# Pacing layer 0 further ahead of layer 1, and giving the ending steps of a tile pair a lower priority number, in a planned two-layer attention kernel

## The chip, the cores and the metric

The kernel runs on one core of one Trainium2 chip. Everything is float32. The metric is the device time of one execution in microseconds (us), as the median of several runs. A core has five instruction queues of interest here: PE (TensorE, matrix products; PEld are its weight loads), ACT (ScalarE, activation functions), DVE (VectorE), POOL (GpSimd) and SP (SyncE, which here only issues DMA transfers). Each queue executes its instructions strictly in the order in which the program issued them; queues wait for each other through semaphores.

## The reference

The input is 8 items (batch) of 64 x 16 positions with 128 channels, that is N = 1024 tokens of C = 128 per item. Two layers follow each other.

```python
# layer 0, per item: attention with 8 heads and two softmaxes in a row, then a feed-forward part
q, k, v = proj(wq), proj(wk), proj(wv)                    # 8 heads of 128
scores  = einsum('bhlfc,bhmgc->bhlfmg', q, k) / sqrt(128) # 1024 x 1024 per head
a = softmax(scores, axis=m); a = softmax(a, axis=g)       # over 64 rows, then over 16 columns
z = a @ v;  z1 = layer_norm(z @ wo.T + bo + x)
x = layer_norm(relu(z1 @ w1.T + b1) @ w2.T + b2 + z1)
# layer 1, per item: additive attention, then a recurrence over the tokens
Bn = ln(t);  Wi = Bn @ W.T
scores[i, j] = sum_d v[d] * tanh(Wi[i, d] + Wi[j, d])     # 1024 x 1024 x 128 tanh
t = t + softmax(scores, axis=j) @ Bn
Wx = batch_norm(ln(t) @ W);  y_t = sigmoid(Wx_t + y_{t-1} @ V.T)
out = t + y
```

Layer 1 of an item needs layer 0 of that item alone; only the batch normalisation and the recurrence at the very end need all 8 items.

## The kernel before, in words

**Two layers at once.** While layer 1 works on item b, layer 0 works on item b + 1. Layer 0 has 64 tiles per item (8 heads x 8 tiles of 128 queries). Tiles go in pairs. For each tile: score products on PE (L856), an exponential on ACT (L859), sums and reciprocals on DVE (L863, L864) and a division on DVE (L867). These *begin* a pair. Once per pair, the *ending* steps follow: one exponential over both tiles on ACT (L876, 128 x 2048), sums and reciprocals on DVE (L879, L880), a division on POOL (L890), four transposes through PSUM banks (L770 on PE, L782 on DVE), the product with the values (L904 on PE) and its addition to `zs` (L909 or L911 on DVE). There are two score buffers, and two pair buffers (`e`, with their statistics `stat_e`).

When the 64 tiles of an item are done, a serial chain ends layer 0: transposes, layer normalisation, the feed-forward part (L944, L950, L957, L963), a second normalisation, for both halves of the tokens. Then layer 1 begins: normalisation, a projection (L1085) and a copy into `wiT` (L1109), one per half.

**Rows.** Layer 1's bulk is `tanh(Wi[i] + Wi[j])` for all i <= j: 36 blocks of 128 x 128 pairs per item, since the scores are symmetric. The rows are made in groups of up to 4096 elements, in one of five slots `th`. A group is either made on ACT by itself (L999, `tanh` with the bias added), or the additions are made on POOL or DVE (L1009, L1003) and ACT applies one `tanh` to the group (L1045). PE multiplies each group by `v` into the tile `sa` (L1062). Block rows 0; 1 and 7; 2 and 6; 3 and 5; 4 are taken in this order (the first and the last item start with 4, 5 and 7, 6 instead, for which half of the tokens is enough). An exponential (L1158) empties `sa` after each, and attention steps with transposes and products (L1191) follow.

**The planner.** Nothing is issued directly. Each step is added to a `Plan` with an engine or several, a modelled duration, the keys that it reads and writes, and a priority number `pri`. `Plan.emit` then replays the program: it finds the earliest time at which any step could start, takes the steps that could start within 0.15 us of that on that engine, and issues the one with the lowest number. Engine order and the division of rows among ACT, POOL and DVE come out of that. The order is fixed when the program is built; the chip only follows it.

**The scale of the numbers.** One unit is one item of layer 1. The rows of item b have `ROWS` from b to b + 1. Layer 0 of item b has the number

```python
def pace(n_part, h):
    return b - 1 - LEAD + STRETCH * (n_part * H + h) / (len(parts) * H)
```

with `STRETCH` 0.95, or 1.25 for the last item. So tile by tile it runs from b - 1 - LEAD upwards: layer 0 of item b is on a par with the rows of item b - 1, `LEAD` units ahead. `L0` is set anew from `pace` for every tile. The chain that ends layer 0 has b - 1 - SOON and layer 1's normalisation and projection have b - SOON, with `SOON` 0.5, so both come ahead of the rows as soon as they can start. The product L1062 and the attention steps of layer 1 have `L1 = ROWS - LEAD`; the tanh of a group has ROWS - 0.02.

The DMAs stand apart: `load_xT` has b - 2, the parking of results follows layer 1's numbers, and `fetch_wx` has NB.

Of the kernel before, what the change touches and what calls it, by code (L numbers as in the profile page):

```python
# [413 lines left out]
class Plan:  # L414
# [24 lines left out]
    def add(self, where, fn, r=(), w=(), pri=0, mode="full", take=None, give=None, behind=(), wait=(), port=False):  # L439
        n = len(self.ops)  # L440
        deps = set()
        for k in r:
            if k in self.writer:
                deps.add(self.writer[k])
        for k in (*w, *wait):
            if k in self.writer:
                deps.add(self.writer[k])
            deps.update(self.readers.get(k, ()))
        for k in w:
            self.writer[k] = n  # L450
            self.readers[k] = []
        for k in r:
            if k not in w:
                self.readers.setdefault(k, []).append(n)
        deps.discard(n)
        self.ops.append((where, fn, (pri, n), mode, deps, take, give, behind, port))
        self.by.append(None)
        return n
# [107 lines left out]
def fast_path(ctx: ExitStack, tc: tile.TileContext, a: dict, fits):  # L566
# [150 lines left out]
    add = plan.add  # L717


    LEAD, SOON, LATE = 0.15, 0.5, -0.3  # L720

    stats = ring("stat", 7, [P, 4, 9])

# [36 lines left out]
    def through_bank(pe, weight, r, evict, where, more, w, pri, choice=two):  # L760

        bank = Bank(*choice)
        n = len(plan.ops)
        add(("PE", weight), lambda _: pe(bank()), r=r, w=[("bank", n)], pri=pri, take=bank, wait=more + w)
        add(where, lambda e: evict(e, bank()), r=[("bank", n)] + more, w=w, pri=pri, give=bank)

    def transposes(srcs):
        def fn(bank):
            for i, s in enumerate(srcs):
                nc.tensor.transpose(bank[:, i * P : (i + 1) * P], s, ident)  # L770

        return fn

    def copy(dst):
        def fn(e, bank):
            src = bank
            if len(dst.shape) == 3:
                src = bank[:, : dst.shape[1] * P].rearrange("p (t c) -> p t c", c=P)
            if e == "ACT":
                nc.scalar.activation(dst, src, AF.Copy)  # L780
            else:
                nc.vector.tensor_copy(dst, src)  # L782

        return fn
# [4 lines left out]
    def layer0(b):  # L789
# [13 lines left out]
        def pace(n_part, h):  # L803
            return b - 1 - LEAD + STRETCH * (n_part * H + h) / (len(parts) * H)

        for n_part, part in enumerate(parts):
# [3 lines left out]
            for h in range(H):  # L810
                L0 = pace(n_part, h)
# [29 lines left out]
                for qt in qts:  # L841
                    L0 = pace(n_part, h + (qt - qts[0]) / len(qts))
# [30 lines left out]


                    ks = [("e", pair, q) for q in range(2)]
                    add(("ACT", 1.9), lambda _, e2=e2: nc.scalar.activation(e2, e2, AF.Exp), r=ks, w=ks, pri=L0)  # L876

                    def second_sums(_, e2=e2, r2=r2):
# [42 lines left out]
            L0 = b - 1 - SOON  # L921
# [53 lines left out]

    def group(it, at0, r0, k, wiT, all_wi, L1, ROWS, fillers, chain, left, both, first_half):

# [80 lines left out]
        def times_v(_):  # L1058
# [15 lines left out]
            ("PE", k * (1.69e-3 * (w - begin[0]) + 0.005 * n)), times_v, r=[("tanh", g)] + before,  # L1074
            w=[("sa", it, r0)] + after, pri=L1, mode="groups", give=slot,
        )
        return ("sa", it, r0)

    def projected(src, ks, w, use, kw, L1, bT, kb):

        through_bank(
            transposes([src[:, i, :] for i in range(4)]), 0.52, ks, copy(bT), ("DVE", 0.7), [], [kb], L1
        )
        through_bank(
            lambda bank: nc.tensor.matmul(bank, w, bT, start=True, stop=True), 0.9, [kb], *use, [], [kw], L1  # L1085
        )
# [8 lines left out]
    def layer1(b):  # L1095
        L1 = b - SOON
        X, kX = Xs[b % NX], ("X", b % NX)
        B, kB = Bs[b % 2], ("B", b % 2)
        wiT, kw = wiTs[b % 2], ("wiT", b % 2)

        early = b in (0, NB - 1)
        for qh in (1, 0) if early else (0, 1):
            Xg, kg = X[:, 4 * qh : 4 * qh + 4, :], kX + (qh,)
            Bg = B[:, 4 * qh : 4 * qh + 4, 0:C]
            layer_norm(Xg, kg, Bg, kB + (qh,), 6, L1)

            def numbered(_, bank, qh=qh):
                dst = wiT[:, 512 * qh : 512 * qh + 512]
                nc.vector.tensor_copy(dst.rearrange("p (t r c) -> p t r c", t=4, c=4), bank.rearrange("p (t c r) -> p t r c", t=4, c=4))  # L1109


            at = wiT[:, 512 * qh : 512 * qh + 512]
            projected(Bg, [kB + (qh,)], wa_sb, (numbered, ("DVE", 0.75)), kw + (qh,), L1, at, kw + (qh,))
        all_wi = [kw + (1,), kw + (0,)]

        E_at = E_first
        fills = [("fill", False), ("fill", True)]
        order = ((4,), (5, 7), (6,), (0,), (1,), (2,), (3,)) if early else shared  # L1120
        done, attended = set(), set()
        past = 0
        for pair in order:
            todo = []
            for it in pair:
                w = N - it * P
                k = max(1, N // w)
                wide = it < NT // 2
                for r0 in range(0, 32, k):
                    late = r0 + 3 * k >= 32  # L1130
                    if wide:
                        fillers = [("ACT", 0.0)] + ([] if late else [("POOL", 0.0)])
                        if b == NB - 1:
                            fillers += [("DVE", 0.1)]
                    elif it == NT // 2:
                        fillers = [("DVE", 0.1), ("ACT", 0.1)] + ([] if late else [("POOL", 0.0)])
                    else:
                        fillers = [("DVE", 0.1)] + ([("ACT", 0.1)] if early else [("POOL", 0.0)])
                    todo.append((r0 + 0.5 * (not wide), it, 0 if it == pair[0] else N - pair[0] * P, r0, k, fillers))
            left = {}  # L1140
            n_blocks = sum(NT - it for it in pair)
            keys = []
            for s, it, at0, r0, k, fillers in sorted(todo):
                ROWS = b + (past + n_blocks * s / 33) / len(E_first) / 4.5
                L1 = ROWS - LEAD
                keys.append(group(it, at0, r0, k, wiT, all_wi[:1] if early and pair[0] >= NT // 2 else all_wi, L1, ROWS, fillers, fills[it < NT // 2], left, fills if r0 == 0 else (), b == 0 and pair[0] >= NT // 2))
            past += n_blocks
            blocks = [("E", it, j) for it in pair for j in range(it, NT)]

            runs = [pair] if not early else [(it,) for it in pair]  # L1150

            def exps(_, runs=runs):
                at0 = 0
                for run in runs:
                    w = sum(NT - it for it in run)
                    Ep = E_sb[:, E_at[run[0]] : E_at[run[0]] + w, :].rearrange("p t (c r) -> p t c r", c=4)
                    S = sa[:, at0 : at0 + w * P].rearrange("p (t r c) -> p t c r", r=32, c=4)
                    nc.scalar.activation(Ep, S, AF.Exp)  # L1158
                    at0 += w * P

            add(("ACT", 0.2 * len(runs) + 0.833e-3 * n_blocks * P), exps, r=["sa"] + keys, w=blocks, pri=L1)
            for it in pair:
                D, kD = E_sb[:, E_at[it], :], ("E", it, it)
                add(("DVE", 0.28), lambda _, D=D: nc.vector.tensor_tensor(D, D, half, ALU.mult),
                    r=[kD], w=[kD], pri=L1, port=True)
                through_bank(
                    transposes([D]), 0.25, [kD],
                    lambda _, bank, D=D: nc.vector.tensor_tensor(D, bank[:, :P], D, ALU.add),
                    ("DVE", 0.3), [kD], [kD], L1,
                )  # L1170
            done.update(pair)
            for it in range(NT):
                if it not in attended and done.issuperset(range(it + 1)):
                    attended.add(it)
                    attention(b, it, X, kX, B, kB, E_at, L1)
# [67 lines left out]
    def check_bounds():  # L1243
# [73 lines left out]
        add(("DVE", 1.7), compared, r=[("at1", 0), ("at1", 1)] + [("ET", j) for j in range(1, NT)], w=["fits"], pri=LATE)  # L1317

    layer0(0)
    check_bounds()  # L1320
    for b in range(NB):
        if b + 1 < NB:
            load_xT(b + 1)
            layer0(b + 1)
        layer1(b)
# [139 lines left out]
```

## Time and profile before

| what | value |
|---|---|
| median of 3 runs (lowest to highest) | 5696.39 us (5690.69 to 5700.09) |
| the profiled execution: its time, and its span | 5699.62 us, 5697.8 us |
| busy: ACT, PE, DVE, POOL (us of the span) | 5263.0, 5166.6, 4754.1, 4186.4 |
| mean granted TensorE clock | 0.975 |
| DMA | 37.82 MB, 7 GB/s in the mean |
| weight loads (PEld) | 2765.7 us, beside PE |

The span is the time from the first to the last instruction; the profiled execution's own time is 1.8 us more. Busy times of different engines overlap. The page also gives, for groups of equal instructions, the number, the busy time, the mean of one, and the idle time of the engine just before them with what ended it. A line number is that of the kernel's source; helpers such as the transposes at L770 are shared by both layers.

### The profile page before, as it was taken

The numbers are of one execution on the slowest core, as the hardware profiler recorded it, in microseconds if no ns is written. First come the engines' busy times: TensorE is split into PE (matmuls) and PEld (weight loads), VectorE is DVE, ScalarE is ACT, GpSimd is POOL, SyncE is SP. The second block draws the span as 40 slices with busy tenths as digits, with TensorE's granted clock in tenths as the row PEclk, the third lists the DMA queues.
The fourth block names the chain that finished last, engine by engine and source line by source line (L and its number), as shares of the span: only waits on it lengthen the run. The fifth ranks groups of instructions, "written<-read, shape, count | busy, mean of one in ns | idle before, by whom it ended". The sixth has DMA issues, their size and how long they took to land.

```text
span 5697.8 us, 97791 instructions
## 1 busy us (share of the span) xinstructions
PE 5166.6 (91%) x39013; PEld 2765.7 (49%) x39013; DVE 4754.1 (83%) x7545; ACT 5263.0 (92%) x4964; POOL 4186.4 (73%) x2678
## 2 busy tenths in 40 slices
PE   8899999899989999899998999989998999987567
PEld 6555455455544555445454455445454445543125
DVE  7989676778996889968898689986899669999886
ACT  5499999999998999899998999989998999999994
POOL 2362997788877888588796888868887886882882
PEclk9999999999999999999999999999999999998988
DMA  2000000000000000000000000000000000000001
GB/s 60 1 5 1 1 1 5 8 1 1 1 5 8 1 1 1 8 5 1 1 5 5 5 1 1 5 8 1 1 1 3 7 1 1 1 21 14 1 1 64
DMA packets 27330, 37.82 MB, mean 7 GB/s; under 512 B 2464, under 2 KB 19232, under 8 KB 26864
## 3 DMA queue, kind: packets, MB, share of 16 engines
q1 hardware_dynamic: 24832, 27.99, 1.5%
q8 instruction: 308, 5.05, 0.4%
q10 hardware_dynamic: 1872, 3.16, 0.2%
q14 instruction: 158, 1.29, 0.1%
q0 software_dynamic: 160, 0.33, 0.1%
HBM read 19.41 MB, written 12.06 MB: 6 GB/s over the span
## 4 chain that ended last, share of the span: by engine, by line
PE 40%; DVE 24%; ACT 23%; issue 4%; POOL 1%; DMA 0%; DVEq 0%; ACTq 0%; POOLq 0%
PE sa L1062 16%; ACT th L1045 10%; ACT th L999 9%; PE m L904 8%; PE sc L856 6%; PE m L770 4%; DVE th L1003 3%; DVE stat_e L879 3%; DVE th L1009 3%; DVE stat_e L863 2%; DVE aT L782 2%; ACT wx L876 2%; DVE wx L867 2%; ACT sc L859 2%; PE m L1191 1%
## 5 line engine op out<-in xcount | busy, mean ns | idle before, releaser
L1009 POOL TENSOR_TENSOR th<-wiT 128x896 f32<-128x896 f32 (+55 forms) x2088 | 3131.7, 1535 | 436.8 <-PE sa L1062 400.4
L1062 PE MATMUL sa<-th,vpat 128*32 128x512 f32 (+27 forms) x24576 | 2104.4, 466 | 223.6 <-ACT th L1045 212.6
L999 ACT ACTIVATE th<-wiT 128x516 f32<-128x516 f32 (+55 forms) x3044 | 2203.1, 798 | 37.1 <-DVE wiT L1109 21.1
L1045 ACT ACTIVATE th<-th 128x4096 f32<-128x4096 f32 (+54 forms) x766 | 2083.8, 2746 | 49.0 <-DVE th L1003 28.0
L890 POOL TENSOR_TENSOR wx<-wx,stat_e 128x1024 f32<-128x1024 f32 x512 | 998.3, 1971 | 755.9 <-DVE stat_e L880 527.5
L1062 PEld LDWEIGHTS sa<-th,vpat 128*32 128x32 f32 x24576 | 674.8, 111 | 1470.4 <-issue 834.4
L856 PE MATMUL sc<-xT,wx 128*128 128x512 f32 x2048 | 985.7, 606 | 36.0 <-DVE wx L867 35.8
L904 PE MATMUL m<-aT,wx 128*128 128x256 f32 x3584 | 862.2, 389 | 14.7 <-DVE aT L782 12.0
L1003 DVE TENSOR_SCALAR_CACHE_REDUCE th<-wiT 128x384 f32<-128x384 f32 (+47 forms) x1092 | 758.1, 694 | 86.3 <-PE sa L1062 15.0
L904 PEld LDWEIGHTS m<-aT,wx 128*128 128x128 f32 x3584 | 660.7, 191 | 238.9 <-issue 89.9
L782 DVE COPY aT<-m 128x512 f32<-128x512 f32 x927 | 598.2, 672 | 138.6 <-PE m L770 136.2
L863 DVE TENSOR_REDUCE stat_e<-sc 128x16 f32<-128x1024 f32 x512 | 620.1, 1211 | 101.1 <-ACT sc L859 99.9
L879 DVE TENSOR_REDUCE stat_e<-wx 128x128 f32<-128x2048 f32 x256 | 583.2, 2278 | 102.5 <-ACT wx L876 101.8
L867 DVE TENSOR_TENSOR wx<-sc,stat_e 128x1024 f32<-128x1024 f32 x512 | 623.4, 1218 | 23.8 <-DVE stat_e L864 0.5
L770 PE MATMUL m<-ident,wx 128*128 128x128 f32 x3932 | 571.9, 280 | 56.7 <-DVE aT L782 29.3
L770 PEld LDWEIGHTS m<-ident,wx 128*128 128x128 f32 x3932 | 434.9, 141 | 357.6 <-issue 164.2
L859 ACT ACTIVATE sc<-sc 128x1024 f32<-128x1024 f32 x512 | 513.1, 1005 | 92.3 <-PE sc L856 76.6
L876 ACT ACTIVATE wx<-wx 128x2048 f32<-128x2048 f32 x256 | 486.8, 1902 | 90.8 <-DVE wx L867 90.8
L856 PEld LDWEIGHTS sc<-xT,wx 128*128 128x128 f32 x2048 | 357.3, 192 | 367.1 <-issue 301.7
L1009 DVE TENSOR_TENSOR th<-wiT 128x1024 f32<-128x1024 f32 (+28 forms) x280 | 392.1, 1439 | 3.9 <-PE sa L1062 3.0
L880 DVE RECIPROCAL stat_e<-stat_e 128x128 f32<-128x128 f32 x256 | 243.9, 953 | 8.8
L738 POOL TENSOR_TENSOR stat<-stat,neg_half 128x4 f32<-128x4 f32 x64 | 65.3, 1020 | 245.4 <-DVE stat L735 230.6
(169 smaller groups left out, 3055.5 us busy)
## 6 DMA issues: line engine op xcount, KB each, us to landing
xT<-in_xt_dram SPq DMA_DIRECT2D x8, 512.0 KB, 3.7
th<-in_x_dram SPq DMA_DIRECT2D x8, 512.0 KB, 7.5
parked<-X SPq DMA_DIRECT2D x16, 256.0 KB, 2.3
xr<-parked SPq DMA_DIRECT2D x8, 512.0 KB, 8.3
parked_wx<-bT SPq DMA_DIRECT2D x14, 256.0 KB, 2.0
wx<-parked_wx SPq DMA_DIRECT2D x7, 512.0 KB, 3.3
out_dram<-ot ACTq DMA_DIRECT2D x8, 256.0 KB, 2.1
out_dram<-ot SPq DMA_DIRECT2D x8, 256.0 KB, 2.2
```

Of the source, the lines that this page charges most:

```text
L770: nc.tensor.transpose(bank[:, i * P : (i + 1) * P], s, ident)
L856: nc.tensor.matmul(sc[:, cols], u[:, qt * P : (qt + 1) * P], xT[:, cols], start=True, stop=True)
L863: nc.vector.tensor_reduce(r1, sc.rearrange("p (m g) -> p g m", g=G), AX.X, ALU.add)
L867: nc.vector.tensor_tensor(e3, sc3, r1.unsqueeze(1).to_broadcast([P, M, G]), ALU.mult)
L879: nc.vector.tensor_reduce(r2, e2.rearrange("p q (m g) -> p q m g", g=G), AX.X, ALU.add)
L890: nc.gpsimd.tensor_tensor(e3, e3, r2[:, q, :].unsqueeze(2).to_broadcast([P, M, G]), ALU.mult)
L904: nc.tensor.matmul(bank()[:, :256], vp[:, t, :], aT[:, t, :], start=t == 0, stop=t == NT - 1)
L999: nc.scalar.activation(rows(c)[:, r, :], wiT[:, i0 + begin[c] :], AF.Tanh, bias=w_i(c, r))
L1003: nc.vector.tensor_scalar(rows(c)[:, r, :], wiT[:, i0 + begin[c] :], w_i(c, r), 0.0, ALU.add, ALU.add, accum_out=unused)
L1009: eng.tensor_tensor(rows(c), wiT[:, i0 + begin[c] :].unsqueeze(1).to_broadcast(shape), w_i(c).unsqueeze(2).to_broadcast(shape), ALU.add,)
L1045: lambda _: nc.scalar.activation(slot()[:, : at[4]], slot()[:, : at[4]], AF.Tanh),
L1062: nc.tensor.matmul(sa[32 * c : 32 * c + 32, s:s1], vpat[:, 31 - r0 - r : 63 - r0 - r], rows(c)[:, r, s - at0 - begin[c] : s1 - at0 - begin ...
```

## The change

Layer 0's pace gets a lead of 0.35 in place of 0.15. Layer 1's products and attention steps keep ROWS - 0.15, now written as a number. The ending steps of a tile pair, from the exponential at L876 on, get a number lower by `DOWN` = 0.06 than the tile that they follow. No instruction is added or removed by the text of the change; the planner decides anew on the order, and on which engine adds which rows.

```diff
-    LEAD, SOON, LATE = 0.15, 0.5, -0.3
+
+    LEAD, DOWN, SOON, LATE = 0.35, 0.06, 0.5, -0.3
...
                     ks = [("e", pair, q) for q in range(2)]
+                    L0 -= DOWN
                     add(("ACT", 1.9), lambda _, e2=e2: nc.scalar.activation(e2, e2, AF.Exp), r=ks, w=ks, pri=L0)
...
                 ROWS = b + (past + n_blocks * s / 33) / len(E_first) / 4.5
-                L1 = ROWS - LEAD
+                L1 = ROWS - 0.15
```

## The prediction

> **What bounds the kernel now.** I read the page first, for the busy shares, then the windows table by stage, then ScalarE's waits and its timeline at one border between items.
>
> The page's first part: ACT and PE are both busy over 90% of the span, and no other engine is.
>
> ```profile
> PE 5166.6 (91%) x39013; PEld 2765.7 (49%) x39013; DVE 4754.1 (83%) x7545; ACT 5263.0 (92%) x4964; POOL 4186.4 (73%) x2678
> ```
>
> ACT is idle for 5697.8 - 5263.0 = 435 us. The windows table says where. Columns: stretch, its length, busy us (and count) of PE, PEld, DVE, ACT, POOL, then clock, DMA share and GB/s. I cut at the borders between items:
>
> ```profile
> 0.00:306.00 306.00, 273.96 (x1239) 190.53 (x1239) 256.33 (x344) 166.33 (x298) 102.24 (x66) 0.99 0.10 28
> ...
> 1200.00:1640.00 440.00, 422.17 (x3421) 226.55 (x3415) 391.96 (x572) 432.92 (x362) 368.60 (x247) 0.99 0.01 2
> 1640.00:1800.00 160.00, 135.91 (x921) 71.47 (x923) 130.07 (x263) 129.82 (x131) 97.71 (x59) 0.94 0.02 8
> 1800.00:2300.00 500.00, 478.98 (x3751) 253.36 (x3749) 425.36 (x593) 493.60 (x404) 429.73 (x275) 1.00 0.00 1
> 2300.00:2480.00 180.00, 155.72 (x1077) 85.34 (x1070) 145.85 (x290) 145.05 (x151) 110.43 (x67) 0.94 0.03 10
> ...
> 5220.00:5600.00 380.00, 236.24 (x2365) 74.03 (x2360) 326.49 (x641) 365.26 (x157) 294.81 (x204) 0.91 0.00 1
> ```
>
> Inside an item ACT is at 98 to 99% and PE at 96%: full. At the borders ACT falls to 81%, PE to 85 to 87%. Over the seven borders (1040:1200, 1640:1800, 2300:2480, 3040:3220, 3690:3840, 4340:4480, 5040:5220) ACT's idle time is 11.4 + 30.2 + 35.0 + 26.6 + 21.1 + 14.6 + 4.5 = 143 us in 1150 us. The stretches between them, from 420 to 5040, leave 61 us idle in 3650 us, or 1.7%. At that rate the borders would have 19 us, so **124 us are lost at the borders**. Before 306 (layer 0 alone, 140 us of ACT idle) and after 5600 (the recurrence, 70 us) lies most of the rest.
>
> ScalarE's waits in the second of these borders, and its timeline there (start, us, engine, line, then the idle time before it and its releaser):
>
> ```profile
> ACT th L999 <- DVE wiT L1109: 15.6, 1, 15.6
> ACT sc L859 <- PE sc L856: 9.2, 2, 7.5
> ACT wx L876 <- DVE wx L867: 6.0, 1, 6.0
> ```
>
> ```profile
> 2407.05 1.90 ACT L876 ACTIVATE wx<-wx 128x2048 f32<-128x2048 f32 x1
> 2416.49 1.01 ACT L859 ACTIVATE sc<-sc 128x1024 f32<-128x1024 f32 x1 [7.53 <-PE sc L856]
> 2433.13 8.40 ACT L999 ACTIVATE th<-wiT 128x1024 f32<-128x1024 f32 x8 [15.63 <-DVE wiT L1109]
> ```
>
> ACT has finished the rows of one item and waits for `wiT` of the next. That is the end of a chain. Counting instructions in the trace for item 2: its last tile exponential (L859) is at 1628, its last addition to `zs` (L911) at 1699, its two `wiT` copies (L1109) at 1718 and 1750; the rows of item 1 (L1062) end at 1734. The chain takes 1750 - 1628 = 122 us, and at its start 106 us of rows were left. In items 3 to 6 it takes 132, 116, 137 and 141 us, with 106, 144, 164 and 154 us of rows left; but ACT, five slots ahead of PE, runs out earlier than PE: at 3066 in the third case, 45 us before the rows end at 3111. DVE is 80% busy in these borders, as layer 0's end and layer 1's own end (normalisations, transposes, attention) fall together.
>
> **The skill.** "SBUF — State Buffer", section "SBUF: two separate sides", says that GpSimd and certain VectorE operations share one port pair as an exclusive lock. The trace agrees: a normalising L742 takes 0.34 us in the median, but four of them take 7.32 us at 1645.92, up to 2.09 us each, where POOL adds rows. It matters since these stand in the chain. "TensorE: Matmul & The Clock Gate", section "Part 1", says that an idle PE lets its clock be gated; here the clock is 0.94 at the borders and 0.99 to 1.00 between, so filling them helps PE a little. "Perfetto Trace Analysis", section "Optimization Strategy", says to find the gaps of the most contended engine within a regime and to make what they wait for start sooner. The gaps shown are of that kind.
>
> **The change, part by part.**
>
> *Lead 0.15 to 0.35.* Rows of items 1 to 6 end at 1734, 2406, 3111, 3787, 4448 and 5070: 667 us per item. 0.2 units are 133 us. Layer 0 follows its pace in the trace (at 900 us it has 1.94 items done with the rows at 0.71, where the pace gives 1.91), so I expect the last tile of an item some 133 us earlier relative to the rows. With 106 to 164 us left now, there would be 239 to 297 us for a chain of 116 to 141 us: `wiT` is ready about 100 to 150 us before the rows end, and ACT's running out 45 us early is covered too. The double buffers (`X`, `B`, `wiT`, `xT`) allow it, since layer 0 of item b + 2 writes `X` only near its end. I take 70% of the 124 us, since layer 1's own end stays with its waits on `sa` and DVE: **-87 us**, bounds -124 and -30. Late next would be L1158 on L1062, 19.9 us in all.
>
> The cost: layer 0 must first get 0.2 units further ahead, and the rows end 0.2 units further behind it. Alone, layer 0 takes about 390 us per item (1.03 items by 400 us); the rows alone 506 us (0.79 item from 5200 to 5600); together 667 us. The shift costs 0.2 x (390 + 506 - 667) = 46 us. ACT can still squeeze rows into the first stretch, so I take **+35 us**, bounds 0 and +46. In the first item layer 0's tiles also pass layer 1's preparation at -0.5 for longer: its rows, from 306 on, may start up to 50 us later, with ACT then about half idle; +25 us at the upper end.
>
> *Down 0.06.* Per pair the steps that move are one ACT exponential (1.90 us), DVE's sums and reciprocal (2.28 + 0.95), two POOL divisions (1.97 each), 16 transposes (0.28 each) with four copies (0.67), 16 products (0.39) and an addition (0.41). 0.06 is four tiles. They already precede the next pair's beginnings, so they only move past layer 1's steps: rows on ACT and POOL, L1062 on PE, attention on DVE. Their work is unchanged; 256 pairs wait less for POOL, whose idle time before L890 is 756 us, and release `e` sooner. ACT and PE stay the full engines, so I take **0**. From below -25: part of ACT's 91 us before L876. From above +50: the exponential is planned as soon as its inputs are ready by the model, and in an in-order queue any lateness of DVE stops the rows behind it, and PE behind those. 0.2 us for each of 256 makes 50.
>
> *Layer 1's numbers* keep ROWS - 0.15: nothing. On SP no transfer changes its number; `load_xT` and the final fetch wait for layer 0, which ends earlier, and the DMA share is under 0.03 there. POOL and DVE get the same row work to share, hidden by POOL's 27% idle time; if a worse division made ACT add some rows itself, a four-row group of 4096 costs ACT 4.2 us by itself (4 x 1.04, from ten L999 at 1753.17) instead of 3.6 (L1045). I take 0, within 20 us either way.
>
> Sum on the profiled execution: 5699.6 - 87 + 35 = 5648 us. The median of the runs is 3.2 us below that execution, so **5645 us**, 0.9% less.
>
> **The rivals.**
>
> *Full recovery:* borders vanish (-110), the start costs 10, the pairs give -25: 5571. For it: the gap at 2417 waits on nothing but `wiT`. Against: DVE is at 80% there, and PE has only 4% to give elsewhere. 0.15.
>
> *The bottleneck moves:* DVE was at 89% in 1200:1640, with its share of narrow rows. Layer 0's end moves into just that stretch, so the borders gain 80 and the stretch loses 20, with 35 for the start: about -35, 5661, at worst no gain. 0.17, and part of it lands within the measurement's bound.
>
> *Slower:* the early exponentials. If L876 waits more than 0.2 us longer in the mean on DVE's L867, 256 x 0.2 = 51 us eat the net gain of 52. At 0.4 us, 102 - 52 = +50: 5746. For it: 35 of 256 already wait, 2.6 us each. Against: most of those are at the borders. 0.2 us is the point from which it decides. 0.17.
>
> *It does not do what it says:* layer 0 cannot get ahead, as DVE already holds it (DVE 256 of 306 us at the start). Then borders stay and so does the time: 5690. 0.06. Against: layer 0 alone ran 1.7 times its shared rate.
>
> **How the numbers follow.** The likeliest case (0.45) is a partial recovery, 5645. 0.2% of the time, about 11 us, is what a measurement here can tell from no change. Faster: 0.45 + 0.15 + two thirds of the second rival and a third of the last, 0.73. Slower 0.17, same 0.10. The range 5572 to 5728 takes in the full recovery and the milder half of the slower case, and leaves out 2 in 10.
>
> **What would show it.** Right: ACT at the borders above 92%, no wait of L999 on L1109 over 3 us, `wiT` copies 100 us before the rows' last L1062; before 600 us ACT less busy; the stretch after layer 0's end longer by about 100 us. Wrong: ACT's wait before L876 above 140 us, or borders as idle as now although `wiT` is early; then DVE, not the chain, made them.

## The result and the profile after

The changed kernel takes **5708.9 us** in the median (5703.11 to 5713.74, 10 runs) against 5696.05 us before (5690.69 to 5700.09, 10 runs): a ratio of 1.0021, with a 95% interval of 1.0013 to 1.0029. It is slower by 0.2%, where 0.9% faster was forecast. The profiled execution has a span of 5703.6 us, 5.8 us more than the one before; the medians are 12.9 us apart.

The page's first part of the changed kernel, in the same columns as before:

```profile
PE 5139.1 (90%) x39013; PEld 2794.3 (49%) x39013; DVE 4804.9 (84%) x7520; ACT 5256.9 (92%) x4900; POOL 4151.8 (73%) x2638
```

ACT works 6 us less and is idle 12 us more. Nothing seems to have happened. The windows table shows otherwise. Rows of items 1 and 2 now end at 1803 and 2481, so the cuts move with them (length, then busy us of PE, PEld, DVE, ACT, POOL):

```profile
1180.00:1710.00 530.00, 499.12 (x3969) 276.16 (x3961) 452.16 (x663) 505.05 (x447) 417.60 (x268) 0.99 0.01 2
1710.00:1870.00 160.00, 144.79 (x937) 78.93 (x941) 131.90 (x210) 144.12 (x119) 125.96 (x72) 0.96 0.02 8
1870.00:2390.00 520.00, 484.70 (x3853) 261.14 (x3849) 462.67 (x642) 493.35 (x423) 421.66 (x272) 0.98 0.01 2
2390.00:2550.00 160.00, 149.01 (x989) 78.97 (x981) 117.98 (x190) 155.24 (x135) 134.07 (x78) 0.97 0.02 7
```

At the two borders ACT is now at 90% and 97%, where it was at 81%. Inside the items it is at 95%, where it was at 98 to 99%. In ScalarE's timeline at the second border no gap is left where the items meet: the exponential that empties `sa` for the last time in item 2 (L1160) is followed at once by a tile exponential and by rows of item 3 (L1001, which was L999):

```profile
2483.09 0.57 ACT L1160 ACTIVATE E<-sa 128x512 f32<-128x512 f32 x1
2483.57 1.00 ACT L860 ACTIVATE sc<-sc 128x1024 f32<-128x1024 f32 x1
2484.51 2.16 ACT L1001 ACTIVATE th<-wiT 128x1014 f32<-128x1014 f32 x2
```

The five longest sums among ScalarE's waits over the whole span (engine, line, awaited engine and line: us in all, times, longest):

```profile
ACT sc L860 <- PE sc L857: 69.2, 57, 4.7
ACT wx L878 <- DVE wx L868: 54.8, 34, 5.9
ACT th L1001 <- PE sa L1064: 45.6, 32, 5.4
ACT th L1047 <- DVE th L1005: 40.9, 44, 2.2
ACT th L1047 <- DVE th L1011: 36.8, 19, 5.5
```

The kernel before had these answers for the same five kinds, and for the wait on `wiT`, which is no longer among ACT's waits:

```profile
ACT wx L876 <- DVE wx L867: 90.8, 35, 11.4
ACT sc L859 <- PE sc L856: 76.6, 54, 8.1
...
ACT th L1045 <- DVE th L1003: 28.0, 24, 2.8
...
ACT th L999 <- DVE wiT L1109: 21.1, 5, 15.6
...
ACT th L1045 <- DVE th L1009: 18.0, 15, 2.6
...
ACT th L999 <- PE sa L1062: 15.4, 10, 4.5
```

So long waits gave way to many short ones: the first two sums and the wait on `wiT` fell, while those for a free slot `th` that PE has not emptied, and for rows that DVE adds, rose. For every kernel below I split ACT's idle time the same way, by its instructions in the trace: *border* is from 90 us before to 70 us after the last L1062 of each of the first seven items; *inside* is the rest from 420 us to the end of the seventh border. Before to after: border 145 to 41 us, inside 57 to 153 us, up to 420 us 142 to 155 us, at the end 76 to 82 us. What the borders gave back, 104 us, the insides lost, 96 us. By what ended it, ACT's idle time at the borders was 64 us for L876 on DVE's L867, 28 us for L859 on PE's L856, and only 21 us for rows on `wiT`; after the change the first of these is 5 us and the third nothing. Inside, L876 on L867 went from 11 to 24 us, the wait for a free slot from 10 to 33 us, and that for rows added by DVE's L1009 (now L1011) from 17 to 37 us.

### The profile page after: what moved, and what is told of

The parts are those of the page before. It is cut to its first block, busy times and chain, and to the rows that moved or that the text cites. A ratio compares the mean times of both kernels' runs of the same rounds, so it can differ in the third digit from the quotient of the medians.

```text
span 5703.6 us, 97886 instructions
## 1 busy us (share of the span) xinstructions
PE 5139.1 (90%) x39013; PEld 2794.3 (49%) x39013; DVE 4804.9 (84%) x7520; ACT 5256.9 (92%) x4900; POOL 4151.8 (73%) x2638
## 4 chain that ended last, share of the span: by engine, by line
PE 43%; DVE 31%; ACT 20%; issue 4%; POOL 1%; DMA 0%; DVEq 0%; SPq 0%; ACTq 0%; POOLq 0%
PE sa L1064 15%; PE m L906 9%; ACT th L1047 8%; PE sc L857 7%; ACT th L1001 7%; PE m L771 5%; DVE th L1005 4%; DVE th L1011 4%; DVE stat_e L881 4%; DVE stat_e L864 3%; DVE wx L868 3%; DVE aT L783 3%; ACT wx L878 2%; ACT sc L860 2%; DVE X L743 1%
## 5 line engine op out<-in xcount | busy, mean ns | idle before, releaser
L1011 POOL TENSOR_TENSOR th<-wiT 128x1024 f32<-128x1024 f32 (+50 forms) x2048 | 3102.4, 1548 | 629.8 <-PE sa L1064 591.0
L1064 PE MATMUL sa<-th,vpat 128*32 128x512 f32 (+33 forms) x24576 | 2089.6, 468 | 253.6 <-ACT th L1047 232.1
L1001 ACT ACTIVATE th<-wiT 128x580 f32<-128x580 f32 (+62 forms) x2992 | 2199.8, 810 | 46.2 <-PE sa L1064 45.6
L1047 ACT ACTIVATE th<-th 128x2250 f32<-128x2250 f32 (+57 forms) x757 | 2082.7, 2774 | 89.0 <-DVE th L1005 40.9
L906 PE MATMUL m<-aT,wx 128*128 128x256 f32 x3584 | 850.3, 390 | 23.3 <-DVE aT L783 17.5
L1005 DVE TENSOR_SCALAR_CACHE_REDUCE th<-wiT 128x309 f32<-128x309 f32 (+50 forms) x1072 | 756.9, 706 | 88.1 <-PE sa L1064 12.1
L906 PEld LDWEIGHTS m<-aT,wx 128*128 128x128 f32 x3584 | 679.6, 194 | 216.0 <-DVE aT L783 49.8
L878 ACT ACTIVATE wx<-wx 128x2048 f32<-128x2048 f32 x256 | 487.0, 1903 | 57.8 <-DVE wx L868 54.8
L1011 DVE TENSOR_TENSOR th<-wiT 128x1024 f32<-128x1024 f32 (+31 forms) x292 | 405.5, 1430 | 7.8 <-PE sa L1064 7.7
L913 DVE TENSOR_TENSOR zs<-m,zs 128x256 f32<-128x256 f32 x215 | 88.0, 409 | 124.6 <-PE m L906 124.1
```

The lines of the kernel that those rows point to most:

```text
L906: nc.tensor.matmul(bank()[:, :256], vp[:, t, :], aT[:, t, :], start=t == 0, stop=t == NT - 1)
L1001: nc.scalar.activation(rows(c)[:, r, :], wiT[:, i0 + begin[c] :], AF.Tanh, bias=w_i(c, r))
L1005: nc.vector.tensor_scalar(rows(c)[:, r, :], wiT[:, i0 + begin[c] :], w_i(c, r), 0.0, ALU.add, ALU.add, accum_out=unused)
L1011: eng.tensor_tensor(rows(c), wiT[:, i0 + begin[c] :].unsqueeze(1).to_broadcast(shape), w_i(c).unsqueeze(2).to_broadcast(shape), ALU.add,)
L1047: lambda _: nc.scalar.activation(slot()[:, : at[4]], slot()[:, : at[4]], AF.Tanh),
L1064: nc.tensor.matmul(sa[32 * c : 32 * c + 32, s:s1], vpat[:, 31 - r0 - r : 63 - r0 - r], rows(c)[:, r, s - at0 - begin[c] : s1 - at0 - begin ...
```

## The experiments

Theories are named as in the expectations. A: the lead gains, the ending steps' lower number costs. B: VectorE's burst at layer 0's end stalls the others wherever it lands. C: the late start of the first rows eats the gain. D: any edit re-deals the planner's order (gives another order among many), and the kernel before is a good draw. E and F, against D: the time follows the pace, and neighbours are alike. G: the burst is only a small part.

**One part alone, a lead between, and a control.** All change one line of the changed kernel:

```diff
-    LEAD, DOWN, SOON, LATE = 0.35, 0.06, 0.5, -0.3
+    LEAD, DOWN, SOON, LATE = 0.35, 0, 0.5, -0.3      # lead alone
+    LEAD, DOWN, SOON, LATE = 0.15, 0.06, 0.5, -0.3   # ending steps alone
+    LEAD, DOWN, SOON, LATE = 0.25, 0, 0.5, -0.3      # a lead between
+    LEAD, DOWN, SOON, LATE = 0.16, 0, 0.5, -0.3      # control
```

> The lead of 0.35 without the lower number of the ending steps (DOWN = 0). Theory A, two effects of opposite sign: the lead gains and the ending steps cost, so about 5665 us (-30 against the kernel before), with ACT's idle time inside the items back near the 6 us per item (from 20% to 80% of the item) that it was before. Theory B, the burst of VectorE work that ends layer 0 stalls ACT wherever it lands, and the lead only moves it: 5700 to 5712 us as the change itself, with ACT idle where layer 0 ends. Theory C, the late first rows (42 us) eat what the borders give: also near 5705, with rows of the first item ending at about 1108 again.

> The ending steps 0.06 lower, with the lead left at 0.15. Theory A: slower than before by 30 to 45 us (5726 to 5741), with more waits of ACT inside the items. Theories B and C: within 8 us of before, 5688 to 5704, with the borders as idle as before (about 144 us in seven).

> A lead of 0.25, DOWN = 0: layer 0 some 67 us further ahead, enough for wiT to be ready about 60 us before the rows end. Theory A: between the others, about 5670 to 5680. Theory B: 5696 to 5705. Theory C: the first item's cost halves (about 20 us) and most of the border gain is kept, so 5680 or better, and better than a lead of 0.35.

> A control: a lead of 0.16, DOWN = 0, which moves layer 0 by 7 us only. If times follow the pace smoothly (A, B, C) it is within 4 us of before (5692 to 5700). Theory D, the planner's order is so sensitive that any edit re-deals the rows and moves the time by 10 to 20 us either way: it lies outside that band, and differences of this size among the others say little.

Each ratio is to the kernel before, timed in the same series, where its median was 5695.8 to 5701.4 us. Lead alone 1.0017 (1.0010 to 1.0024), ending steps alone 1.0058 (1.0045 to 1.0072), lead 0.25 0.9978 (0.9969 to 0.9987), and the control, which moves layer 0 by 7 us, **1.0081** (1.0067 to 1.0095), or 45 us. A, B and C alike had allowed the control 4 us. Only D named a time outside that band, and its 10 to 20 us were too small as well. It also takes the force out of the others: the lead alone (5710.7 us) fell where B said, the ending steps alone (5733.4 us) where A said, and the lead of 0.25 (5687.7 us) where none did, but a single difference of 30 us between two orders says little on the edit.

**Neighbours of both paces.** The same line, with other leads:

> A lead of 0.14, DOWN = 0: with 0.15 and 0.16 a third order at nearly the same pace. Theory D (every edit re-deals the order, and the kernel before is a good draw among its neighbours): slower than before, 5710 to 5750 us. Theory E (0.16 is the unlucky one and the time otherwise follows the pace): within 6 us of the kernel before.

> A lead of 0.17, DOWN = 0, a fourth order at nearly the same pace. Theory D: slower than before, 5710 to 5750 us. Theory E: within 6 us of the kernel before, or up to 5 us faster by the trend to 0.25.

> The changed kernel with 0.34 in place of 0.35. Theory D: anywhere from 5680 to 5740 us, and with its neighbours' mean below that of the leads near 0.15, since the borders' idle time is gone in all of them. Theory E: within 6 us of the changed kernel.

> The changed kernel with 0.36 in place of 0.35. Theory D: anywhere from 5680 to 5740 us. Theory E: within 6 us of the changed kernel.

> A lead of 0.34, DOWN = 0. Theory D: within about 20 us of the 5711 us that 0.35 gave, on either side; the mean over 0.34, 0.35 and 0.36 without DOWN below that with it if the ending steps' lower number costs anything (the pair at 0.15 said +32 us, but of a single draw). Theory E: within 6 us of 5711.

> A lead of 0.36, DOWN = 0. Theory D: within about 20 us of 5711 us, on either side. Theory E: within 6 us of it.

> A lead of 0.24, DOWN = 0. If a lead of about 0.25 is better in itself (theory C: the borders covered with half the cost at the start), 5680 to 5697 us. If 0.25 was a good draw only (theory D), around 5705 to 5730 us.

> A lead of 0.26, DOWN = 0. Theory C: 5680 to 5697 us. Theory D without a better middle: around 5705 to 5730 us.

The results are in the table below. E falls near 0.15: 0.14 and 0.17 are slower by 0.6 and 1.9%, the latter (5807.6 us) beyond what D named too. It is not excluded everywhere: without DOWN, 0.34, 0.35 and 0.36 agree within 5 us by their ratios, and 0.24 and 0.25 within 3 us. C is not borne out: 0.24 and 0.25 are faster than before, but 0.26, for which C had 5680 to 5697 us, took 5708.8 us, 0.27% more than the kernel before, so that group's mean is that of the kernel before.

**The order dealt anew, nothing else.** Neighbouring leads still differ in pace. So the planner's slack, the 0.15 us within which it compares numbers, was moved by 0.001 us. No pace, number or modelled duration changes; the issued order does, on every engine, and with it the division of rows among the engines (POOL has 2726 instructions with 0.151 at the old pace, where it had 2678).

```diff
-    def emit(self, slack=0.15, switch=0.1, stay=0.015):
+    def emit(self, slack=0.151, switch=0.1, stay=0.015):   # and 0.149
```

> The kernel before with the planner's slack at 0.151 us in place of 0.15: no pace, priority or duration changes, only ties fall otherwise. Theory D (the kernel before is a good draw of order): 5710 to 5760 us. Theory F (the neighbours at 0.14, 0.16 and 0.17 are slower because of their pace): within 8 us of the kernel before.

> The kernel before with the planner's slack at 0.149 us, a third order at the same pace. If the kernel before is a good draw, as the slack of 0.151 said, 5710 to 5760 us; if the slack itself matters in one direction, faster than before.

> The changed kernel with the planner's slack at 0.151 us. Theory D: 5680 to 5715 us, the spread that 0.34, 0.35 and 0.36 showed. Theory F: within 8 us of the changed kernel.

> The changed kernel with the planner's slack at 0.149 us, a third order at its pace: 5685 to 5725 us as a draw from the spread seen so far, and below the slack of 0.149 with the old pace by some 30 us if the new pace is better in the mean.

At the old pace 1.0062 (1.0045 to 1.0079) and **1.0128** (1.0111 to 1.0145): 31 and 73 us slower for no change of intent. At the new pace 1.0044 and 1.0051, that is 13 and 17 us slower than the changed kernel. F falls, and D holds in kind: the order alone moves the time by more than most of the differences above. Three of the four times lie beyond D's ranges, all to the slow side, by 2 to 10 us. With the slacks of 0.151 and 0.149 the new pace beats the old by 8 us (5722.1 against 5729.7) and by 43 us (5726.8 against 5770.2); with 0.15 it loses 13 us. In the mean of the three that is about 13 us faster, from draws that scatter more than that.

The orders at the new pace are also not wholly independent. By the traces, the changed kernel with 0.151 keeps the order of the changed kernel on ACT, DVE and POOL up to about 2957 us, half of the span; at the old pace the orders with other slacks part from the kernel before by 85 and 391 us. So the smaller spread at the new pace may in part come from shared order. The waits of ScalarE in the order with 0.149 at the old pace show some of what the kernel before was spared:

```profile
ACT th L999 <- DVE wiT L1109: 78.6, 4, 34.1
ACT sc L859 <- PE sc L856: 73.1, 59, 6.0
ACT th L1045 <- DVE th L1003: 49.5, 41, 5.3
```

The wait on `wiT` that the prediction took for the typical loss is 78.6 us in this order, with the longest 34.1 us; in the kernel before it is 21.1 us. ACT's wait before L876 went the other way, to 42.9 us from 90.8.

All orders together (idle times of ACT in us, from the profiled executions):

| lead, DOWN, slack | ratio to before (95%) | ACT idle inside | border | last row of item 0 at |
|---|---|---|---|---|
| 0.15, 0, 0.15 (before) | 1 | 57 | 145 | 1066 |
| 0.15, 0, 0.151 | 1.0062 (1.0045-1.0079) | 98 | 136 | 1080 |
| 0.15, 0, 0.149 | 1.0128 (1.0111-1.0145) | 106 | 151 | 1110 |
| 0.14, 0, 0.15 | 1.0058 (1.0039-1.0078) | 77 | 161 | 1087 |
| 0.16, 0, 0.15 | 1.0081 (1.0067-1.0095) | 103 | 151 | 1087 |
| 0.17, 0, 0.15 | 1.0189 (1.0168-1.0210) | 146 | 169 | 1107 |
| 0.15, 0.06, 0.15 | 1.0058 (1.0045-1.0072) | 92 | 136 | 1086 |
| 0.24, 0, 0.15 | 0.9983 (0.9976-0.9990) | 103 | 56 | 1116 |
| 0.25, 0, 0.15 | 0.9978 (0.9969-0.9987) | 106 | 63 | 1114 |
| 0.26, 0, 0.15 | 1.0027 (1.0015-1.0039) | 102 | 90 | 1101 |
| 0.34, 0, 0.15 | 1.0009 (1.0002-1.0016) | 102 | 81 | 1112 |
| 0.35, 0, 0.15 | 1.0017 (1.0010-1.0024) | 113 | 72 | 1117 |
| 0.36, 0, 0.15 | 1.0009 (1.0000-1.0018) | 148 | 42 | 1120 |
| 0.34, 0.06, 0.15 | 0.9983 (0.9976-0.9990) | 131 | 45 | 1111 |
| 0.35, 0.06, 0.15 (after) | 1.0021 (1.0013-1.0029) | 153 | 41 | 1108 |
| 0.36, 0.06, 0.15 | 0.9996 (0.9986-1.0005) | 120 | 54 | 1111 |
| 0.35, 0.06, 0.151 | 1.0044 (1.0027-1.0061) | 157 | 54 | 1105 |
| 0.35, 0.06, 0.149 | 1.0051 (1.0034-1.0067) | 147 | 63 | 1118 |

At leads of 0.14 to 0.17 without DOWN the mean of six is 1.0086 (standard error 0.0027); with the five of the changed kernel's kind it is 1.0019 (0.0013). The difference is -0.67%, with a standard error of 0.30, or about -38 us. With so few orders the 95% interval runs from -1.4% to 0.0%. All eleven orders with a lead of 0.24 or more, against all seven with 0.14 to 0.17, give -0.7% (-1.3 to -0.1), so that a larger lead is faster in the mean is fairly well supported; how much of it the lead of 0.35 with DOWN gives is not. These intervals take the orders as independent draws. The kernel before lies 0.86%, or 49 us, below the mean of its own group: it is the fastest of the six.

**Less of VectorE's burst, the order kept.** The gains are one and the biases zero in these inputs, so 80 products and additions at the end of layer 0 can go without a change in the output. Their modelled durations stay, and with them the order, instruction for instruction. Done to the kernel before and to the changed kernel:

```diff
-                layer_norm(Xg, kg, Xg, kg, qh, L0, affine1)
+                layer_norm(Xg, kg, Xg, kg, qh, L0, lambda: None)
...
-                    nc.vector.tensor_tensor(Xg, Xg, over_tiles(b2_sb, 4), ALU.add)
+                    pass
...
-                layer_norm(Xg, kg, Xg, kg, 2 + qh, L0, affine2)
+                layer_norm(Xg, kg, Xg, kg, 2 + qh, L0, lambda: None)
```

> The kernel before with its planned order kept instruction for instruction, but without the 80 VectorE additions and products of the gains and biases in the chain that ends layer 0 (L930, L931, L964, L967, L968; gains are one and biases zero in these inputs). Some 80 us of VectorE's busy time go. Theory B (the burst of VectorE work is what stalls the others where it lands): 30 to 60 us faster. Theory G (what stalls is the order as a whole, the burst only a part): 5 to 25 us faster.

> The changed kernel, likewise without these 80 VectorE instructions and with its order kept. Theory B: 20 to 50 us faster, as the burst now stalls the inside of the items. Theory G: under 15 us faster, since the lead hides the chain.

Before: 5636.63 us, ratio 0.9890 (0.9874 to 0.9907), 62 us less. Changed: 5646.46 us, 0.9909 (0.9893 to 0.9926) to the kernel before, which is 64 us less than its own 1.0021. Both pass the upper end of what B named; G falls. In the traces ACT, DVE and POOL run the same instructions in the same order as without the edit, less the 80 of DVE. The pages' first parts, the kernel before without these instructions first, then the changed one without them:

```profile
PE 5160.7 (92%) x39013; PEld 2762.8 (49%) x39013; DVE 4672.4 (83%) x7465; ACT 5260.6 (93%) x4964; POOL 4182.9 (74%) x2678
```

```profile
PE 5128.4 (91%) x39013; PEld 2784.5 (49%) x39013; DVE 4738.4 (84%) x7440; ACT 5254.3 (93%) x4900; POOL 4142.0 (73%) x2638
```

DVE is relieved by 4754.1 - 4672.4 = 82 us and by 4804.9 - 4738.4 = 67 us; ACT's busy time stays. The 80 instructions themselves had taken 76 and 78 us in the two kernels, so about 0.8 us comes off the time for each us of them, though DVE's share of the span is 83 to 84%, and though the changed kernel has `wiT` more than 100 us early. ACT's idle time goes where the chain lies: before, border 145 to 97 us and inside 57 to 45; after, inside 153 to 102 us and border 41 to 38. The edit shortens the chain as well as DVE's work, and leaves fewer DVE instructions to meet GpSimd's; no run takes these apart.

In the changed kernel DVE and ACT are both 92% busy in the stretch in which layer 0 of item 2 ends:

```profile
1541.00:1700.00 159.00, 145.51 (x1247) 81.96 (x1245) 146.76 (x308) 146.90 (x152) 109.19 (x83) 0.97 0.02 5
```

In the kernel before, the same chain (first line) has DVE at 89% and ACT at 75%, and a stretch without a chain (second line) has DVE at 93% with ACT at 99%. So DVE's busy share in a stretch does not by itself say whether ACT stalls; the runs with less work on it do.

```profile
1640.00:1760.00 120.00, 98.24 (x649) 52.49 (x649) 107.05 (x226) 89.82 (x102) 61.37 (x38) 0.91 0.02 5
...
1400.00:1600.00 200.00, 194.49 (x1630) 105.00 (x1623) 185.35 (x316) 198.71 (x165) 166.78 (x120) 1.00 0.01 1
```

## Why the prediction was wrong

**Right: the chain and its cover.** An earlier chain was forecast by 133 us, with `wiT` ready 100 to 150 us before the rows end. Over items 1 to 6 it is ready 117 us before, in the mean, where it was 6 us; the wait of ACT on L1109 is gone. The term "-87" for the borders was if anything too small: their idle time fell by 104 us. The signs of being right that the prediction named came true as far as they concern the borders (ACT at 96% over all seven) and `wiT`; none of them looked inside the items. Its account of the borders rests on one of them, though: over all seven, only 21 of ACT's 145 idle us were direct waits on `wiT`, and 64 were L876 waiting on DVE's L867. (By time most of ACT's wait before L876 was at the borders, as it said, but not by count: 12 of 35.) While `wiT` is late, ACT has no rows to put into such a wait, so the chain can stand behind these too; that they went when the chain came early fits this, but no run separates it from DVE's load. The help it expected for PE's clock is not there: 0.96 and 0.97 at the two borders, but 0.98 to 0.99 inside, and 0.971 over the span, where it was 0.975.

**Wrong: that the inside of an item stays as it is.** This is the step that failed: the sum had no term for it. The prediction read ACT's 1.7% between the borders as what any order gives there; on the profiled executions the inside lost 96 us. The runs put two things in its place.

First, 57 us inside belonged to this one order. Five other orders at leads of 0.14 to 0.17 have 77 to 146 us, mean 106, with their borders as idle as before (136 to 169 us). The new order did not keep it. Whether the kernel before has a favourable order by luck, or because its constants were once picked by their time, no run shows. Against the mean of its group it is 49 us fast, and that is nearly what the change was to bring. The difference of the group means, -38 us, lies near the forecast of 52 us less, but its interval reaches zero; the measured difference compares one draw with another. The same holds for the start: rows of item 0 ended 42 us later, as the +35 said, but five other orders at the old leads end them at 1080 to 1110, mean 1094. The mean of the five changed orders, 1111, is 16 us later than that, so less than half of the 42 us is shown to be due to the pace. In idle time of ACT the cost term "+35" was 13 us up to 420 us and 6 us at the end.

Second, the cost of the chain's burst moved with the chain. This was the second rival ("the bottleneck moves"), whose "stretch loses 20" was too small. (Its own sum is off too: 80 gained less 20 and 35 makes -25, not -35.) The runs with the order kept show it: the 80 instructions cost the kernel before 48 us of ACT's idle time at the borders and 12 inside, and the changed kernel 3 at the borders and 51 inside. A covered wait was forecast to be free; DVE's work behind it was not. The groups agree less sharply: ACT's idle time inside is 120 to 157 us in the five orders of the changed kind, mean 142, against 98 over all six at the old pace. But with a lead of 0.34 and 0.35 and no DOWN it is only 102 and 113, with 81 and 72 left at the borders. So how much idle time moves inside depends on the order, and perhaps on DOWN.

**Right: the ending steps are worth about nothing.** At a lead of 0.34 to 0.36 the three orders with DOWN have a mean ratio of 1.0000, the three without 1.0012. At 0.15 the single order with DOWN (1.0058) lies within the spread of those without it. A cost of 30 to 45 us, as theory A had it, is not seen.

**The slower rival named the wrong thing.** It said that L876 would wait longer on L867 and gave 140 us as the mark. That wait fell from 90.8 to 54.8 us, though inside the items it rose from 11 to 24 us. The sign came out on its side for another reason.

Not settled is how an order gains 50 us inside. The waits involved are many and short, and no single instruction was shown to carry them. Among the seven orders at 0.14 to 0.17 the granted clock of PE tends to be lower where the time is longer, from 0.975 in the fastest to 0.965 in the slowest; no run shows whether it is a cause or follows from PE's waits.

Three orders are faster than both kernels: leads of 0.25 and 0.24 without DOWN and 0.34 with it, by 0.17 to 0.22% against the kernel before. They are the best of the eighteen; the one at 0.26, slower than the kernel before, shows that a lead near 0.25 alone does not bring it.

## What to carry to other kernels

Where a planner fixes the order, compare groups of orders, not two of them: re-deal both sides with an edit that means nothing, and look at the spread before reading a small difference. A stretch that runs at 99% may be a draw rather than the rule. When three engines are above 80%, idle time of the fullest one that leaves one stretch may come back in another; ask what work made it, and take that work away with the order held fixed to see its price. Choose the signs that will show you right or wrong in every stretch, not only where the gain is expected.

## What the runs showed of the hardware

One program repeats closely: ten runs of the kernel before lie within 9.4 us, and 48 in a later series within 17.8 us. Another order of the same work, with a parameter moved by 0.001 us, lies up to 73 us away. The queues kept the order that they were given when the timing changed: in the kernel before without the 80 instructions, ACT (4964 instructions), POOL (2678) and DVE (7465) ran theirs in the same order as with them, in 62 us less.

The same VectorE instruction has no one price here. The 16 products of L930, all 128 x 512, in the kernel before (shortest, median, longest in ns), and one of the longest in the timeline:

```profile
L930 DVE TENSOR_TENSOR X<-X,ln_g_sb x16: 691/1082/2201, 233.0 to 5162.5; 128x512 f32<-128x512 f32 x16
...
1653.27 2.20 DVE L930 TENSOR_TENSOR X<-X,ln_g_sb 128x512 f32<-128x512 f32 x1
```

The trace tells the two kinds apart, and it fits the exclusive port lock that the prediction cites. Eight of the products met no GpSimd instruction and took 691 to 693 ns. The other eight began while a GpSimd row addition (L1009) was running, 150 to 159 ns after its start; they took 1470 to 2201 ns, and each ended 545 to 551 ns after that addition ended. In the changed kernel three did so (549 to 553 ns after), while three that began before an addition took 691 to 692 ns beside it. The copy L1109 from PSUM to `wiT` took 627 to 692 ns beside GpSimd work or without it. No run took GpSimd's work away, so this rests on the order of events in the traces.
